# Rounding through int16 and int8 in a fused cross-attention and ternary FFN layer, with W_down prepared apart and a re-planned instruction order

## The chip, the cores and the metric

One NeuronCore of a Trainium2 chip runs the whole kernel. The metric is the device time in microseconds (us) of one execution. PE is the matmul engine, PEld its weight loads, DVE the vector engine, ACT the scalar engine, POOL the GpSimd engine, SP the engine that issues all transfers of this kernel.

## The reference

For each of 32 batches `x[b]` (128x512) and a context of the same shape, all float32:

```
x = x + xattn(layernorm(x), ctx)      # 8 heads; scores 512x512 per head, RoPE on half of each head
x = x + ffn(layernorm(x))             # 512 -> 2048 -> 512

act_quant(v):    s = 128 / clip(max|v|, 1e-5);   clip(round(v*s), -128, 127) / s     # per token
weight_quant(w): s = 1 / clip(mean|w|, 1e-5);    clip(round(w*s), -1, 1) / s         # ternary
ffn(x) = bitlinear(fwht(silu(bitlinear(x, w_gate)) * bitlinear(x, w_up)), w_down)
bitlinear(x, w) = act_quant(x) @ weight_quant(w).T                                   # fwht: Hadamard over 2048
```

Attention treats the 128 rows as channels and the 512 columns as positions, so one batch has 8 heads of 512x512 scores. Rounding is to the nearest integer in three places: the two activation quantizations and the three weights (1 MB of float32 per quarter, 4 MB each).

## The kernel before: work, staging and order

The work of a batch is cut into some thirty generators (`s_load`, `s_a`, ... `s_dn`), each of which yields what it needs next: a buffer ("get"), an event ("on"), or an engine with an estimated duration. `Plan.run` plays all generators against each other when the program is built: it keeps a clock for every engine, and among the steps that could start first on an engine it takes the one of lowest rank, given by the table `CFG` (one number per generator for the middle batches, one with `.h` for the first four and one with `.z` for the last four, plus `T` per batch). [...] Transfers, all on SP's one queue, have a length and a latency there (`DMA`, and the numbers behind `yield "dma"`). `Plan` also keeps DVE steps marked `"port"` and POOL steps from overlapping in its own clock.

Per batch, the attention runs as two units of four heads. For each unit PE makes eight groups of scores for the row maxima (`s_mpe`, L726), which DVE reduces (`s_mdve`, L741); the maxima go to DRAM and back as extra rows of the query tile (L772, L777); PE makes the scores again, transposed and with the maxima subtracted (`s_epe`, L796); ACT takes the exponential (`s_eact`, L809), and PE multiplies by the values (`s_eav`, L830). The score buffers `pS` and `pT` exist once each. The unit's sums go through DRAM, are normalized (`s_o`, L939 on POOL), projected (L948) and added to `x` (L880).

The FFN: `s_o2` normalizes, quantizes (L975 and L978) and transposes; `s_gpe`/`s_upe` multiply by W_gate and W_up (L1013); `s_gact` (silu, L1043), `s_udve` (L1068) and `s_bf` (butterflies on POOL, L1097) follow, then transposes (`s_zt`, L1117), a split into a high and a low part (`s_hi` L1129, `s_lo` L1140) and the last Hadamard factor (`s_hm`, L1156/L1157). `s_yv` copies to SBUF (L1171), `s_am` finds the token maximum (L1184 to L1223), `s_q` scales on POOL (L1232), `s_q1` and `s_q2` round (L1242, L1256), and `s_dn` multiplies by W_down (L1274) and adds the residual (L1280).

How before rounds: adding 12582912 to a float32 number leaves it rounded to an integer, and a later step takes the constant off again.

```
975   nc.scalar.activation(w, l2, AF.Identity, bias=MAG, scale=sx)             # w in PSUM
978   nc.vector.tensor_scalar(xq, w, -MAGIC, 127.0, ALU.add, ALU.min)
1242  nc.scalar.activation(y, y, AF.Identity, bias=MAG)
1256  nc.scalar.activation(s["yq"][:, w], s["y"][:, w], AF.Relu, bias=MAG7, scale=-1.0)
1275  nc.tensor.matmul(ps, NEG, CS, start=False, stop=True)
```

L1256 holds 127 minus the rounded value, so that one Relu clips it; L1275 takes the shift of 127 out of the product with W_down's column sums `CS`, made once in `s_w4` (16 matmuls at L502, four small DVE steps and a transfer to the two rows of `CS`).

The weights are prepared while the first batches' attention runs. `s_w` loads twelve pieces of 128x2048 (1 MB, L438) into the FFN's own buffers `z0`, `z1`, `z0`, `y`. `s_w1` sums absolute values in halves (L451, all on ACT), `s_w2` scales and adds the constant (L475 on ACT, one on POOL at L477), `s_w3` clips on DVE (L485), `s_w4` takes the constant off and writes fp8 on ACT (L493). The first FFN matmul (L1013 of batch 0) waits until all three weights are ready; the first L1274 waits for `CS`.

Of the kernel before, what the change touches and what calls it, by code (L numbers as in the profile page):

```python
# [13 lines left out]
F8 = mybir.dt.float8e4  # L14
AF = mybir.ActivationFunctionType
# [5 lines left out]
MAGIC = 12582912.0  # L21
EPS = 1e-5
# [3 lines left out]
    "a": 17204.8,  # L26
    "a.h": 56888.9,
    "a.z": 14936.6,
    "a2": 4110.6,
    "a2.h": 10733.7,  # L30
    "a2.z": 4091.9,
    "a3": -1064.4,
    "a3.h": 4876.9,
    "a3.z": 2422.1,
    "am": 4773.1,
    "am.h": 13803.0,
    "am.z": -44218.1,
    "bf": 3144.9,
    "bf.h": 24712.8,
    "bf.z": 19590.3,  # L40
    "const": 14934.4,
    "const.h": 15491.8,
    "const.z": 4076.0,
    "dn": 4293.7,
    "dn.h": 4871.1,
    "dn.z": 21179.4,
    "eact": -36632.4,
    "eact.h": -37814.4,
    "eact.z": -1863.9,
    "eav": 11135.5,  # L50
    "eav.h": 4223.8,
    "eav.z": 32251.8,
    "epe": -40145.6,
    "epe.h": -40187.6,
    "epe.z": -39869.7,
    "gact": 23899.5,
    "gact.h": -26090.9,
    "gact.z": -36563.3,
    "gpe": 56880.8,
    "gpe.h": 18311.9,  # L60
    "gpe.z": 6005.8,
    "hi": -25784.5,
    "hi.h": -26246.1,
    "hi.z": 4960.2,
    "hm": -21491.6,
    "hm.h": -24541.6,
    "hm.z": -28755.2,
    "init": -37791.2,
    "init.h": -23577.8,
    "init.z": -24582.5,  # L70
    "lo": 1897.6,
    "lo.h": 4758.2,
    "lo.z": -37078.3,
    "load": 23789.4,
    "load.h": 4770.3,
    "load.z": -31350.6,
    "mdve": 1736.2,
    "mdve.h": 4251.6,
    "mdve.z": -25448.7,
    "mfin": -25604.8,  # L80
    "mfin.h": 4075.5,
    "mfin.z": 6355.4,
    "mpe": -26070.7,
    "mpe.h": -37503.9,
    "mpe.z": -21599.3,
    "o": -25785.8,
    "o.h": 35362.7,
    "o.z": -786.3,
    "o2": -37005.1,
    "o2.h": -41684.7,  # L90
    "o2.z": -24211.2,
    "q": 13848.2,
    "q.h": -39189.8,
    "q.z": 4318.1,
    "q1": 11956.7,
    "q1.h": 4753.0,
    "q1.z": 21160.0,
    "q2": 1023.0,
    "q2.h": -21667.4,
    "q2.z": -23754.1,  # L100
    "st": -47909.0,
    "st.h": -35889.1,
    "st.z": 21989.2,
    "u": 26418.5,
    "u.h": 5310.5,
    "u.z": 24337.0,
    "udve": 18718.4,
    "udve.h": 12493.6,
    "udve.z": -34405.8,
    "upe": 29615.8,  # L110
    "upe.h": 19928.1,
    "upe.z": 14589.9,
    "v": 27752.8,
    "v.h": 57650.1,
    "v.z": 53459.6,
    "w": 35469.7,
    "w.h": -19469.2,
    "w.z": 18308.4,
    "w1": 24353.6,
    "w1.h": 18083.3,  # L120
    "w1.z": -34718.8,
    "w2": 28388.6,
    "w2.h": 5547.9,
    "w2.z": 12473.5,
    "w3": 31248.0,
    "w3.h": 19526.9,
    "w3.z": 3962.9,
    "w4": 25647.7,
    "w4.h": 6555.5,
    "w4.z": 20517.4,  # L130
    "yv": -26156.9,
    "yv.h": 11959.1,
    "yv.z": 33180.6,
    "zt": 13824.7,
    "zt.h": 15480.3,
    "zt.z": -26679.3,
    "T": 5.6,
    "eps": 0.019,
    "pen": 9.6,
    "stick": 4685.6,  # L140
    "epspe": 0.21,
# [5 lines left out]
    "xq": 1, "xqT": 2, "pf": 3, "z0": 2, "z1": 1, "hl": 2, "y": 1, "yq": 2, "ot": 1,  # L147
# [155 lines left out]
def xattn_ffn(  # L303
# [37 lines left out]
    MAG = const.tile([128, 1], F32, name="MAG")  # L341
    nc.vector.memset(MAG, MAGIC)
    NMAG = const.tile([128, 1], F32, name="NMAG")
    nc.vector.memset(NMAG, -MAGIC)
    MAG7 = const.tile([128, 1], F32, name="MAG7")
    nc.vector.memset(MAG7, MAGIC + 127.0)
# [10 lines left out]
    CW = const.tile([128, 388], F32, name="CW")  # L357
    WQ, WK, WVT, BRP, MASK = CW[:, 0:128], CW[:, 128:256], CW[:, 256:384], CW[:, 384:386], CW[:, 386:387]
    NEGC = CW[:, 387:388]
# [15 lines left out]

    ob = const.tile([128, 1], BF, name="ob")
    nc.vector.memset(ob, 1.0)
    NEG = const.tile([2, 128], BF, name="NEG")
    CS = const.tile([2, 512], BF, name="CS")
# [30 lines left out]
    def s_init():  # L410
        yield "on", "cw"
        yield "dve", 0.2
        nc.vector.tensor_scalar(NEG, ones[0:2, :], NEGC[0:2], None, ALU.mult)
        z = zeros[:, :, None].to_broadcast([128, 2, T])
        for i in range(4):
            yield ("dve", "pool"), (1.13, 1.4), "port"
            E[p.eng].tensor_scalar(kss[i], z, MASK, None, ALU.add)
            p.mark("ks", i)
# [10 lines left out]
    WR = ("z0", "z1", "z0", "y")  # L429

    def s_w():
        for n in range(12):
            m, k = divmod(n, 4)
            src = srcs[m][0][k]
            yield "get", WR[n % 4]
            yield "dma", 2.9
            w = fp.tile([128, 2048], F32, name=WR[n % 4], bufs=2 if WR[n % 4] == "z0" else 1)
            nc.sync.dma_start(out=w.rearrange("p (j i) -> p j i", j=4) if m == 2 else w, in_=src)  # L438
            WT[n] = w
            p.marks["w", n] = p.done  # L440
            p.now = p.done - 2.9

    def s_w1():
        for m in range(3):
            for n in range(4 * m, 4 * m + 4):
                yield "on", "w", n
                for h in range(2):
                    yield ("act", "dve"), (1.1, 1.13)
                    w, a = WT[n][:, bass.ts(h, 1024)], acc[:, 2 * n + h : 2 * n + h + 1]
                    if p.eng == "act":  # L450
                        nc.scalar.activation(AB, w, AF.Abs, accum_out=a)  # L451
                    else:
                        nc.vector.tensor_reduce(a, w, AX.X, ALU.add, apply_absolute_value=True)
            yield "get", "pf"
            yield "pe", 0.1
            pw = ps_f.tile([128, 512], F32, name="pf")
            nc.tensor.matmul(pw[:, 0:8], ones, acc[:, 8 * m : 8 * m + 8], start=True, stop=True)
            yield "dve", 0.1
            sw = SW[:, m : m + 1]
            nc.vector.tensor_reduce(sw, pw[:, 0:8], AX.X, ALU.add)  # L460
            p.put("pf")
            yield "dve", 0.1
            nc.vector.tensor_scalar(sw, sw, 1.0 / (NI * 128 * 512), EPS, ALU.mult, ALU.max)
            yield "dve", 0.1
            nc.vector.reciprocal(SC[:, m : m + 1], sw)
            p.mark("sw", m)

    def s_w2():
        for n in range(12):
            m = n // 4  # L470
            yield "on", "sw", m
            yield ("act", "pool", "dve"), (1.95, 2.7, 1.25), "port"
            w = WT[n]
            if p.eng == "act":
                nc.scalar.activation(w, w, AF.Identity, bias=MAG, scale=SC[:, m : m + 1])  # L475
            else:
                E[p.eng].tensor_scalar(w, w, SC[:, m : m + 1], MAGIC, ALU.mult, ALU.add)  # L477
            p.mark("w2", n)

    def s_w3():  # L480
        for n in range(12):
            yield "on", "w2", n
            yield ("dve", "pool"), (1.2, 2.7), "port"
            w = WT[n]
            E[p.eng].tensor_scalar(w, w, MAGIC - 1.0, MAGIC + 1.0, ALU.max, ALU.min)  # L485
            p.mark("w3", n)

    def s_w4():
        for n in range(12):
            m, k = divmod(n, 4)  # L490
            yield "on", "w3", n
            yield "act", 1.95
            nc.scalar.activation(srcs[m][1][:, k, :], WT.pop(n), AF.Identity, bias=NMAG, saturate=False)  # L493
            p.put(WR[n % 4])
            if k == 3:
                p.mark("wr", m)
        yield "get", "y"
        yield "get", "pf"
        yield "pe", 3.5
        pc = ps_f.tile([128, 512], F32, name="pf")  # L500
        for j in range(NI):
            nc.tensor.matmul(pc[0:1, :], ob, WDQ[:, j, :], start=(j == 0), stop=(j == NI - 1))  # L502
        yield "dve", 0.6
        w = fp.tile([128, 2048], F32, name="y")
        ca, cb = w[0:1, 0:512], w[0:1, 512:1024].bitcast(BF).rearrange("p (a f) -> p a f", a=2)
        nc.vector.tensor_scalar(ca, pc[0:1, :], 1.0 / 64.0, MAGIC, ALU.mult, ALU.add)
        yield "dve", 0.6, "port"
        nc.vector.tensor_scalar(cb[:, 0], ca, -MAGIC, None, ALU.add)
        yield "dve", 0.6, "port"
        nc.vector.tensor_scalar(ca, ca, -MAGIC, -64.0, ALU.add, ALU.mult)  # L510
        yield "dve", 0.6
        nc.vector.tensor_tensor(cb[:, 1], pc[0:1, :], ca, ALU.add)
        p.put("pf")
# [503 lines left out]
    def s_gpe():  # L1017
        for b in range(NB):
# [3 lines left out]
            if b == 0:  # L1022
                yield "on", "wr", 2
# [330 lines left out]
```

## Time and profile before

| | us |
|---|---|
| median of 3 runs (lowest to highest) | 1439.01 (1437.6 to 1448.16) |
| the profiled execution, its whole time | 1444.41 |
| its span, first to last instruction | 1442.5 |
| PE busy | 1353.4 (94%) |
| ACT busy | 1189.0 (82%) |
| DVE busy | 1179.0 (82%) |
| POOL busy | 994.7 (69%) |
| moved by transfers | 214.15 MB, mean 148 GB/s |

How to read it: "busy" is the time an engine executes instructions. The tables by stage give this for stretches of the span, with the mean clock that was granted to PE (1.00 is full speed). In the lists of waits a line names the instruction that waited, the one that ended the wait, the total, how many times, and the longest. In a timeline a row is one instruction or a run of them: start, length, engine, line, operation, output<-inputs, shapes, count.

### The profile page before, as it was taken

To read this page: it belongs to the slowest core of one execution; us is meant where nothing else is said; L and a number is where in the kernel's file an instruction comes from. 1 tells how busy PE (TensorE), PEld (TensorE's weight loads), DVE (VectorE), ACT (ScalarE), POOL (GpSimd) and SP (SyncE) were. 2 spreads that over 40 slices of the span, in tenths; PEclk is the share of its full clock that TensorE was granted. 3 is DMA by queue.
4 is the path that set the end of the run, shared out by engine and by line. 5 is a ranking of instruction groups with operands and counts; after the bars stand their busy time and mean duration, and the time that the engine had idled before them with its cause. 6 is when DMAs were issued, how large, how long until landed. Compare 5 with 4: busy or idle time off the path is not lost.

```text
span 1442.5 us, 21845 instructions
## 1 busy us (share of the span) xinstructions
PE 1353.4 (94%) x7454; PEld 529.8 (37%) x7454; DVE 1179.0 (82%) x1759; ACT 1189.0 (82%) x1574; POOL 994.7 (69%) x781
## 2 busy tenths in 40 slices
PE   3788899999999999999999999999999999999875
PEld 2222233433334333333333344333333343433332
DVE  2875878888898889888888888888888888886784
ACT  5688978888888888888888888888888888889643
POOL 3122229977777777887777787887777788769550
PEclk7596899999999999999999999999999999999986
DMA  8967555555445555555545555555554554321000
GB/s 285 282 201 245 158 159 160 151 152 143 134 147 163 171 171 174 161 153 148 136 134 154 171 167 175 168 162 156 137 141 140 161 166 153 95 65 49 21 15 15
DMA packets 136315, 214.15 MB, mean 148 GB/s; under 512 B 36746, under 2 KB 38924, under 8 KB 135180
## 3 DMA queue, kind: packets, MB, share of 16 engines
q1 hardware_dynamic: 136204, 212.75, 49.7%
q8 instruction: 59, 0.97, 0.3%
q14 instruction: 52, 0.43, 0.1%
HBM read 106.94 MB, written 93.31 MB: 139 GB/s over the span
## 4 chain that ended last, share of the span: by engine, by line
PE 84%; DVE 7%; ACT 4%; DMA 2%; issue 2%; POOL 0%; SPq 0%; ACTq 0%; DVEq 0%; POOLq 0%
PE pav L830 17%; PE pf L1013 15%; PE pT L796 14%; PE pS L726 10%; PE pf L1274 8%; PE pf L1117 4%; PE pf L556 4%; PE pf L1156 3%; ACT P L809 2%; DVE M L741 2%; PE pf L1157 2%; PE pf L948 2%; PE pf L636 2%; DVE ya L1184 1%; PE pf L1275 1%
## 5 line engine op out<-in xcount | busy, mean ns | idle before, releaser
L741 DVE TENSOR_REDUCE M<-pS 128x2 f32<-128x1024 f32 x488 | 595.0, 1219 | 105.0 <-PE pS L726 103.1
L1097 POOL TENSOR_TENSOR z<-z 128x512 f32<-128x512 f32 x491 | 619.0, 1283 | 68.5 <-DVE z L1068 48.5
L809 ACT ACTIVATE P<-pT 128x1024 f32<-128x1024 f32 x512 | 523.2, 1022 | 148.2 <-PE pT L796 146.4
L830 PE MATMUL pav<-P,va 128*32 128x512 f32 x2048 | 283.6, 625 | 0.0
L796 PE MATMUL pT<-qs,ks 50*128 50x512 f32 x1024 | 259.0, 500 | 17.1 <-ACT P L809 16.5
L726 PE MATMUL pS<-ks,qs 48*128 48x512 f32 x976 | 227.2, 458 | 14.8 <-DVE M L741 9.9
L796 PEld LDWEIGHTS pT<-qs,ks 50*128 50x128 f32 x1024 | 98.1, 188 | 240.3 <-ACT P L809 149.9
L1232 POOL TENSOR_TENSOR y<-y,YB 128x1024 f32<-128x1024 f32 x60 | 140.9, 2369 | 34.9 <-ACT YB L1218 34.9
L1013 PEld LDWEIGHTS <-xqT 128*128 128x128 bf16 x1024 | 91.8, 100 | 155.7 <-issue 84.8
L726 PEld LDWEIGHTS pS<-ks,qs 48*128 48x128 f32 x976 | 95.3, 190 | 117.8 <-issue 39.6
L532 POOL TENSOR_TENSOR arstd<-arstd,MHALF 128x1 f32<-128x1 f32 x32 | 18.6, 580 | 170.4 <-DVE arstd L529 134.8
L1013 PE MATMUL pf<-WGQ,xqT 128*128 128x512 fp8e4 x512 | 133.4, 386 | 1.0 <-ACT z L1043 0.6
L1274 PE MATMUL pf<-WDQ,yq 128*128 128x512 fp8e4 x512 | 125.4, 389 | 8.6 <-ACT yq L1256 8.5
L1184 DVE TENSOR_REDUCE ya<-y 128x128 f32<-128x1024 f32 x64 | 127.1, 1986 | 6.6 <-ACT y L1171 6.3
L1013 PE MATMUL pf<-WUQ,xqT 128*128 128x512 fp8e4 x512 | 127.0, 381 | 0.1
L1068 DVE TENSOR_TENSOR z<-z,pf 128x512 f32<-128x512 f32 x128 | 84.6, 675 | 12.9 <-PE pf L1013 8.7
L1140 DVE TENSOR_TENSOR lo<-pf,hi 128x512 fp32r<-128x512 f32 x128 | 85.7, 675 | 6.0 <-ACT hi L1129 5.9
L1043 ACT ACTIVATE z<-pf,tk 128x512 f32<-128x512 f32 x128 | 83.7, 685 | 7.4 <-PE pf L1013 4.7
L1129 ACT CAST hi<-pf 128x512 fp32r<-128x512 f32 x128 | 74.6, 588 | 17.9 <-PE pf L1117 17.9
L1171 ACT COPY y<-pf 128x512 f32<-128x512 f32 x128 | 71.9, 585 | 13.6 <-PE pf L1157 13.3
L1117 PE MATMUL pf<-CM,z 128*128 128x128 f32 x512 | 82.0, 286 | 0.0
L1274 PEld LDWEIGHTS <-yq 128*128 128x128 bf16 x512 | 46.1, 99 | 89.7 <-ACT yq L1256 22.5
(129 smaller groups left out, 1791.5 us busy)
## 6 DMA issues: line engine op xcount, KB each, us to landing
xd<-X SPq DMA_DIRECT2D x128, 512.0 KB
qs<-xd SPq DMA_DIRECT2D x128, 192.0 KB
ks<-xd SPq DMA_DIRECT2D x128, 192.0 KB
ud<-U SPq DMA_DIRECT2D x62, 256.0 KB
xt<-x SPq DMA_DIRECT2D x32, 256.0 KB
ct<-cx SPq DMA_DIRECT2D x32, 256.0 KB
RR<-R SPq DMA_DIRECT2D x64, 128.0 KB
xr<-x SPq DMA_DIRECT2D x32, 256.0 KB
```

The costliest lines, as they stand in the source:

```text
L726: nc.tensor.matmul(ps[e], qs[w, t, bass.ts(qt, 128)], ks[w, t, :], start=True, stop=True)
L741: nc.vector.tensor_reduce(m, ps[2], AX.X, ALU.max)
L796: nc.tensor.matmul(ps[:, e], ks[w, t, bass.ts(kt, 128)], qs[w, t, :], start=True, stop=True)
L809: nc.scalar.activation(P, TQ[u, n], AF.Exp, scale=0.25)
L830: nc.tensor.matmul(av[32 * h : 32 * h + 32, :], va[:, kt, 4 * hf + h, :], P[:, e], start=(kt == 0), stop=(kt == 3),)
L1013: nc.tensor.matmul(ps, xqT[:, k, :], W[:, k, bass.ts(c, 512)], start=(k == 0), stop=(k == 3))
L1097: E[p.eng].tensor_tensor(ix(dv, k), ix(av, 0), ix(av, 1), o)
L1117: nc.tensor.transpose(ps[:, i, :], st[b]["z"][:, bass.ts(4 * c + i, 128)], EYE)
L1140: nc.vector.tensor_tensor(t, F.pop(("z", b, c)), F["hi", b, c].bitcast(F32), ALU.subtract)
L1184: nc.vector.tensor_reduce(ya[:, h], s["y"][:, 8 * h : 8 * h + 8].rearrange("p j t -> p t j"), AX.X, ALU.max, apply_absolute_value=True,)
L1232: E[p.eng].tensor_tensor(y, y, st[b]["YB"].to_broadcast([128, 8, 128]), ALU.mult)
L1274: nc.tensor.matmul(ps, s["yq"][:, j, :], WDQ[:, j, :], start=(j == 0), stop=False)
```

## The change

Rounding is left to the conversion that an engine makes when it writes an integer type.

- `s_o2`: ACT writes `l2*sx` as int16 into SBUF (`xi`), DVE clips it from there to bf16. The PSUM buffer between them goes.
- `s_q1`, `s_q2`: ACT copies `y` to int16 (`yi`, a new buffer, one), which frees `y` there; DVE, no longer ACT, clips `yi` to `yq` in bf16.
- `s_dn`: L1275, `NEG`, `CS` and all that made them go; `s_am`'s last factor changes sign.
- Weights: three steps become two: scale to int8 (`w_scale`; all 14 on ACT in the built order) and clip from int8 to fp8 (`w_clip`, on DVE). The int8 pieces lie in the two halves of the `yi` buffer. W_gate and W_up are loaded into `z0`, `z1`, `z0` and, in two halves, into the `yq` buffers. W_down goes through `y` alone, and twice: four loads for the sum of absolute values, four again for scaling (eight loads of 1 MB in place of four).
- The first FFN matmul waits for W_gate and W_up alone, the first L1274 for W_down. `yi` is handed to batch 0 when all weights are done.
- All of `CFG` has new numbers, a `wd` entry and other `T`, `eps`, `pen`, `stick`, `epspe`; the lengths and latencies behind many `yield "dma"` are larger. So the order of instructions differs on every engine, from the first transfers on.

```diff
-MAGIC = 12582912.0
-    "T": 5.6, "eps": 0.019, "pen": 9.6, "stick": 4685.6, "epspe": 0.21,
+    "T": 573.1, "eps": 0.239, "pen": 38.0, "stick": 11286.1, "epspe": 0.192,
...
+    WP = [(m, k, 0, 2048, r) for m in range(2) for k, r in enumerate(("z0", "z1", "z0"))]
+    WP = [x for m in range(2) for x in WP[3 * m : 3 * m + 3] + [(m, 3, 1024 * h, 1024, "yq") for h in range(2)]]
...
+    def w_scale(w, wi, m, n):
+        yield ("act", "dve", "pool"), (0.2 + 0.88 * n / 1024, 0.15 + 1.07 * n / 1024, 0.3 + 2.7 * n / 1024), "port"
+        if p.eng == "act":
+            nc.scalar.activation(wi, w, AF.Identity, scale=SC[:, m : m + 1])
+        else:
+            E[p.eng].tensor_scalar(wi, w, SC[:, m : m + 1], None, ALU.mult)
+
+    def w_clip(wi, o, n):
+        yield "dve", 0.1 + 1.0 * n / 1024
+        nc.vector.tensor_scalar(o, wi, 1.0, -1.0, ALU.min, ALU.max, saturate=False)
...
+    def s_wd():
+        yield "on", "st", 1
+        for n in range(8):
+            ph, k = divmod(n, 4)
+            yield "get", "y"
+            yield "dma", 3.5
+            w = fp.tile([128, 2048], F32, name="y", bufs=1)
+            nc.sync.dma_start(out=w.rearrange("p (j i) -> p j i", j=4), in_=srcs[2][0][k])
+            p.now = p.done
+            if ph:
+                yield "on", "wi"
+                yield "get", "wi"
+                wi = WI.pop(0)
+                yield from w_scale(w, wi, 2, 2048)
+                p.put("y")
+                yield from w_clip(wi, srcs[2][1][:, k, :], 2048)
+                WI.append(wi)
+                p.put("wi")
+            else:
+                yield from abs_sum(w, 16 + 2 * k, 2048)
+                p.put("y")
+            if n == 3:
+                yield from scale(2)
+        p.mark("wr", 2)
+        yield "on", "wr", 1
+        p.put("yi")
...
-            yield "get", "pf"
-            yield "act", 0.75
-            w = ps_f.tile([128, 512], F32, name="pf")
-            nc.scalar.activation(w, l2, AF.Identity, bias=MAG, scale=sx)
-            yield "dve", 0.6
+            yield "act", 0.6
+            xi = xp.tile([128, T], I16, name="xi", bufs=1)
+            nc.scalar.activation(xi, l2, AF.Identity, scale=sx)
+            p.put("l2")
+            yield "dve", 0.35, "port"
             xq = xp.tile([128, T], BF, name="xq", bufs=1)
-            nc.vector.tensor_scalar(xq, w, -MAGIC, 127.0, ALU.add, ALU.min)
+            nc.vector.tensor_scalar(xq, xi, 127.0, None, ALU.min)
...
             if b == 0:
-                yield "on", "wr", 2
+                yield "on", "wr", 1
             yield "get", "z0"
...
-                nc.scalar.activation(y, y, AF.Identity, bias=MAG)
+                nc.scalar.copy(st[b]["yi"][:, w], st[b]["y"][:, w])
                 p.mark("q1", b, hf)
+            p.put("y")
...
-                yield "act", 1.05
+                yield "dve", 0.45, "port"
...
-                nc.scalar.activation(s["yq"][:, w], s["y"][:, w], AF.Relu, bias=MAG7, scale=-1.0)
+                nc.vector.tensor_scalar(s["yq"][:, w], s["yi"][:, w], 127.0, None, ALU.min)
...
             if b == 0:
-                yield "on", "cs"
+                yield "on", "wr", 2
...
-                    nc.tensor.matmul(ps, s["yq"][:, j, :], WDQ[:, j, :], start=(j == 0), stop=False)
-            nc.tensor.matmul(ps, NEG, CS, start=False, stop=True)
+                    nc.tensor.matmul(ps, s["yq"][:, j, :], WDQ[:, j, :], start=(j == 0), stop=(j == NI - 1))
```

## Prediction

> **What bounds the kernel now.** I read the page's busy times and slices first, then the table by stage, the waits of the stretch in which PE has gaps, and PE's timeline in the steady part.
>
> ```profile
> PE 1353.4 (94%) x7454; PEld 529.8 (37%) x7454; DVE 1179.0 (82%) x1759; ACT 1189.0 (82%) x1574; POOL 994.7 (69%) x781
> ...
> PE   3788899999999999999999999999999999999875
> ...
> PEclk7596899999999999999999999999999999999986
> ```
>
> PE is the bound from about 200 us to 1320 us. Outside of that it has gaps, and early on a granted clock below full. The stages (PE, PEld, DVE, ACT, POOL busy, then clock, transfer share, GB/s):
>
> ```profile
> 0.00:40.00 40.00, 15.93 (x66) 8.27 (x67) 13.06 (x34) 25.27 (x34) 13.05 (x17) 0.72 0.85 292
> ...
> 80.00:100.00 20.00, 16.67 (x100) 5.71 (x98) 16.75 (x27) 17.68 (x23) 5.06 (x4) 1.00 0.43 131
> 100.00:120.00 20.00, 15.30 (x79) 5.60 (x79) 14.04 (x20) 18.75 (x21) 5.51 (x5) 0.82 0.96 314
> 120.00:140.00 20.00, 17.43 (x71) 4.45 (x65) 6.98 (x10) 15.02 (x21) 7.06 (x6) 0.50 0.66 214
> 140.00:160.00 20.00, 16.51 (x93) 6.06 (x91) 16.80 (x25) 18.16 (x23) 1.83 (x2) 0.91 0.74 243
> 160.00:180.00 20.00, 15.69 (x79) 4.49 (x75) 15.28 (x21) 18.20 (x18) 7.41 (x5) 0.83 0.36 80
> 180.00:200.00 20.00, 18.06 (x89) 6.59 (x87) 14.11 (x23) 14.49 (x16) 1.81 (x2) 0.83 0.73 218
> 400.00:440.00 40.00, 40.00 (x236) 15.80 (x232) 35.03 (x52) 34.70 (x48) 31.89 (x26) 1.00 0.52 155
> 1320.00:1360.00 40.00, 34.57 (x168) 12.87 (x167) 22.45 (x41) 28.70 (x38) 28.28 (x22) 0.91 0.14 43
> 1360.00:1400.00 40.00, 32.80 (x146) 15.27 (x144) 33.64 (x54) 24.36 (x35) 20.48 (x14) 0.91 0.02 8
> ```
>
> In the steady part PE has no gap and the others have 5 us or more in 40. From 80 to 200 us PE is idle 120 - 99.66 = 20.3 us while ACT is busy over 18 of 20 us in three of six stretches: it carries the weights' steps beside the exponentials. Who ended PE's waits there (the list for 100 to 150 us, then for 150 to 200 us; columns: total us, times, longest):
>
> ```profile
> PEld pT L796 <- ACT P L809: 16.4, 13, 2.2
> ...
> PE pT L796 <- ACT P L809: 7.3, 8, 1.3
> ```
>
> ```profile
> PEld pS L726 <- DVE M L741: 11.4, 10, 2.0
> ...
> PEld pT L796 <- ACT P L809: 8.6, 10, 2.0
> ...
> PE pS L726 <- DVE M L741: 4.3, 5, 1.7
> PE pT L796 <- ACT P L809: 3.8, 4, 1.7
> ```
>
> ACT's exponentials end 16.4 + 7.3 + 8.6 + 3.8 = 36.1 us of these waits. DVE's maxima end 11.4 + 4.3 and 4.6 in three small rows (1.8, 1.7, 1.1), 20.3 in all. ACT's share is 36.1 / 56.4 = 0.64.
>
> **The change part by part.** The sum is made against the profiled execution: 1444.41 us, of which 1442.5 are span; the median of the runs is 5.4 us below it.
>
> *L1275.* PE's timeline in the steady part:
>
> ```profile
> 473.90 1.90 PE L1274 MATMUL pf<-WDQ,yq 128*128 128x512 fp8e4 x8
> 475.74 0.38 PE L1275 MATMUL pf<-CS,NEG 2*128 2x512 bf16 x1
> 476.05 0.50 PE L796 MATMUL pT<-qs,ks 50*128 50x512 f32 x2
> ```
>
> From its start to the next start are 0.31 us; eight matmuls followed by L796 take 1.83 us elsewhere too (L1013 at 503.09, next at 504.92), as the eight L1274 do here. So 32 x 0.31 = 10.0 us of a full PE go. The order of the other matmuls changes as well. I priced every group in both orders by the start-to-start intervals of its kind and neighbours between 210 and 1320 us: 1326.6 us before, 1319.9 after. So the new mix of switches gives back 10.0 - 6.7 = 3.3 us; bounds 0 and 6.7 (for over a quarter of the groups the new neighbours do not occur in the trace, and kinds alone priced them). A batch then takes 39.8 us in place of 40.13.
>
> *CS.* L502 stands on the chain of waits for 3.54 us at 188.18: 3.5 us go; its four DVE steps (0.7, 0.7, 0.4, 0.4 us), the transfer of 2 KB and five memsets of 0.06 us lie beside PE work.
>
> *q2 moves.* ACT loses 64 x 1.138 us (L1256), 2.3 per batch, and gains nothing: the int16 write of L1242 and of L975 is priced at their rows (1.138, 0.769). ACT is under PE by 5 us per 40, so this gives 0 in the steady part. DVE gains two clips. The trace has no int16; the nearest form is L485 (SBUF to SBUF, one scalar step, 1.21 us for 2048), so 0.61 for 1024, between 0.27 (L768, the smallest tensor step) and 1.22 (L1232 on DVE). L978 (0.68, from PSUM) becomes 0.3 by the same rate. DVE per batch: 35.1 + 1.2 - 0.4 = 35.9 of 39.8: room of 3.9 us. Behind each clip the next L741 is queued, and PE's L726 waits for that one, since `pS` exists once. In the new steady order PE has at least 1.7 us from one pS group to the next, the same as in the old order, which ran without a gap. So I take 0, with that room as the cover.
>
> By the table of modes in the Trainium skill (VectorE: DVE Perf Modes, the section on cycles for N=2048) an all-16-bit clip of 1024 would take an estimated 0.43 us, DVE 35.6 per batch; the sum would be the same.
>
> *A lock that speaks against it.* POOL's R step took 2.16 us at 176.66, where it takes 1.27 otherwise, while L485 held DVE:
>
> ```profile
> 176.47 1.22 DVE L485 TENSOR_SCALAR z<-z 128x2048 f32<-128x2048 f32 x1
> ```
>
> ```profile
> 175.31 1.27 POOL L662 TENSOR_TENSOR RR<-RR,ROPE 128x512 f32<-128x512 f32 x1
> 176.66 2.16 POOL L664 TENSOR_TENSOR R<-R,RR 128x512 f32<-128x512 f32 x1
> ```
>
> So a clip from SBUF and a POOL step exclude each other. The old steady part has no such DVE step; the new one has three per batch beside a POOL that is busy 31.9 of 40. Waiting for the rest of a POOL step, 0 to 1.28 us each (2.37 behind L1232), adds 0 to 3 x 1.28 = 3.8 us per batch to DVE: just inside its 3.9. I take the half, 1.9, hidden.
>
> The Trainium skill (SBUF, "Who interferes with whom") says the later of the two blocks for the whole instruction, an int16 clip included. By it all three could wait a whole POOL step, and DVE would stand at 39.7 of 39.8, nearly a second bound; by the half it costs nothing.
>
> *The start.* CW, ROPE and CM now precede x, three pieces of W_gate precede RR in place of two, and the first piece of W_up precedes the first score tiles. Ahead of the last transfer of unit 0's tiles stand 11.3 MB in place of 9.8 (sizes of the issue list). At 292 GB/s the 1.5 MB cost 5.1 us on the chain to the first scores, where PE has nothing else: +5; bounds 0 (the chain R to X sets it) and 9 (projection later too).
>
> *80 to 200 us.* Of the weights' steps ACT has from 95 us on 8 x 2.0 (L493), 6 x 2.09 (L475) and 8 x 1.24 (L451), 38.5 us. In the new order only W_down's sums (9.9) and four scalings (8.4) are left there, 18.3: ACT loses 20 of 105 us. The clips to fp8 are DVE's: 12 x 1.21 by L485, up to 12 x 2.44 by L1232, most of them done by the second unit; before, it had 12 x 1.26 there. Nothing is priced for DVE here at the lower price. PE gets back ACT's share of its idle time, 0.64 x 20.3 = 13 us; bounds 0 (DVE or transfers are late next) and 20.3. W_down's four extra MB cost 4 / 0.29 = 14 us of a queue that is idle 47 us between 40 and 200 us: hidden, unless it stands ahead of a small transfer (3.6 us per MB). Batch 0's L1156 waits for `y`, that is for W_down's eighth load; if it comes late PE stands up to 3.6 + 2.1 us, and `yi` holds batch 0's L1242 until all weights are done, on ACT with exponentials behind it. The order puts the last scaling 41 ACT places ahead of that, so 0.
>
> *The tail.* On the last batch's chain L1256's second half gets 0.5 shorter and L978 0.4: -1; its new order may give or take 6.
>
> Sum: -10.0 + 3.3 - 3.5 + 5 - 13 - 1 = -19.2, or 1425 for the profiled execution. On the median: 1439.0 - 19.2 = 1420.
>
> **The rivals.** (a) Transfers, not ACT, hold the early attention: the share is 0.96 at 100 to 120 us, and 4 MB come on top. Against it: 0.36 and 0.43 in two stretches with the same PE idle time. Then 13 is not gained and the start costs 9: 1420 + 13 + 4 = 1437. (b) The lock decides in the steady part: each of three waits costs PE half a POOL step, 0.64 us, as L741 comes late: 3 x 0.64 x 29 batches = 56, 1476. It decides from 19.2 / 29 = 0.7 us of PE gap per batch. For it: POOL's share; against: DVE's room. (c) More comes back: all of 20.3, and the half clock at 120 to 140 us, which cost 17.43 / 2 = 8.7, by ACT's share 5.6: 1420 - 7 - 6 = 1407.
>
> **How the numbers follow.** Forecast 0.50 (1410 to 1430), (a) 0.22, (b) 0.13, (c) 0.15. About 1% (1424.6 to 1453.4) is what a measurement tells from no change. The forecast lies under 1424.6 in 0.44 of its 0.50, with (c) 0.59, rounded to 0.6 faster; the rest of it and (a) make 0.27 the same, (b) 0.13 slower. The range runs from all terms at their good ends, 1439 - 10 - 3.5 - 20.3 - 6 = 1399, to (a) with the tail's 6 and L1156's 5.7 on top, 1449.
>
> **What would show it.** Right: steady batches of 39.8 us (L1274 to L1274), PE at 40.00 of 40; idle PE from 80 to 200 us near 7 us and fewer us of "pT <- ACT P"; first L726 near 42 in place of 37 us. Wrong: "pS <- DVE M" growing in the steady part with clips longer than 0.6 us, or PE's early waits going from ACT to DVE or to transfers.

## The result

The changed kernel takes 1460.3 us (median of 4 runs, 1459.18 to 1461.71), the kernel before 1441.27 us beside it (4 runs, 1437.6 to 1448.16): a ratio of 1.0127, 95% interval 1.0085 to 1.0169. It is slower by 1.3%, where 1420 us were forecast. The profiled execution took 1460.03 us, with a span of 1457.2.

### The profile page after: what moved, and what is told of

It is laid out like the page before. It is cut to its first block, busy times and chain, and to the rows that moved or that the text cites. A ratio compares the mean times of both kernels' runs of the same rounds, so it can differ in the third digit from the quotient of the medians.

```text
span 1457.2 us, 21717 instructions
## 1 busy us (share of the span) xinstructions
PE 1340.4 (92%) x7406; PEld 532.5 (37%) x7406; DVE 1242.0 (85%) x1819; ACT 1113.1 (76%) x1501; POOL 999.9 (69%) x777
## 4 chain that ended last, share of the span: by engine, by line
PE 70%; DVE 15%; ACT 8%; DMA 3%; issue 2%; POOL 1%; SPq 0%; ACTq 0%; DVEq 0%; POOLq 0%
PE pav L842 14%; PE pf L1023 13%; PE pT L808 12%; PE pS L738 8%; PE pf L1291 7%; DVE M L753 5%; ACT P L821 4%; PE pf L1127 3%; PE pf L1166 3%; DVE yq L1273 3%; PE pf L648 2%; PE pf L1167 2%; PE pf L960 2%; PE pf L568 1%; DMA RR<-R 1%
## 5 line engine op out<-in xcount | busy, mean ns | idle before, releaser
L1194 DVE TENSOR_REDUCE ya<-y 128x128 f32<-128x1024 f32 x64 | 126.3, 1974 | 13.1 <-ACT y L1181 10.8
L1023 PEld LDWEIGHTS <-xqT 128*128 128x128 bf16 x1024 | 86.2, 98 | 131.8 <-issue 61.2
L1291 PE MATMUL pf<-WDQ,yq 128*128 128x512 fp8e4 x512 | 123.9, 387 | 4.6 <-DVE yq L1273 3.2
L671 POOL TENSOR_TENSOR R<-R,ROPE 128x512 f32<-128x512 f32 x32 | 41.9, 1309 | 71.0 <-DMA RR<-R 71.0
L1181 ACT COPY y<-pf 128x512 f32<-128x512 f32 x128 | 74.1, 582 | 14.2 <-PE pf L1167 13.8
L1139 ACT CAST hi<-pf 128x512 fp32r<-128x512 f32 x128 | 74.2, 586 | 11.7 <-PE pf L1127 10.8
L1127 PEld LDWEIGHTS pf<-CM,z 128*128 128x128 f32 x512 | 59.0, 147 | 54.0 <-issue 33.3
```

The source lines that it names most:

```text
L1023: nc.tensor.matmul(ps, xqT[:, k, :], W[:, k, bass.ts(c, 512)], start=(k == 0), stop=(k == 3))
L1127: nc.tensor.transpose(ps[:, i, :], st[b]["z"][:, bass.ts(4 * c + i, 128)], EYE)
L1194: nc.vector.tensor_reduce(ya[:, h], s["y"][:, 8 * h : 8 * h + 8].rearrange("p j t -> p t j"), AX.X, ALU.max, apply_absolute_value=True,)
L1291: nc.tensor.matmul(ps, s["yq"][:, j, :], WDQ[:, j, :], start=(j == 0), stop=(j == NI - 1))
```

## The profile after the change

The page's busy times and slices, as the prediction showed them of the kernel before:

```profile
PE 1340.4 (92%) x7406; PEld 532.5 (37%) x7406; DVE 1242.0 (85%) x1819; ACT 1113.1 (76%) x1501; POOL 999.9 (69%) x777
...
PE   3698899998999999999999999999999999999775
...
PEclk7579999998999999999999999999999999999997
```

PE is busy 13 us less and the span is 14.7 us longer, so PE's idle time grew by 28 us. The mean granted clock over the whole span is the same (0.953, before 0.950); it is lower in the stretch from 200 to 480 us and higher ahead of it. DVE's busy time went up by 63 us and ACT's down by 76. Two rows of the table by stage (PE, PEld, DVE, ACT, POOL busy, then clock, transfer share, GB/s):

```profile
120.00:140.00 20.00, 16.67 (x101) 5.31 (x93) 10.12 (x18) 16.48 (x22) 5.58 (x5) 0.91 0.91 270
...
400.00:440.00 40.00, 37.98 (x201) 15.50 (x198) 32.38 (x45) 30.87 (x41) 25.01 (x21) 0.91 0.51 150
```

By the six rows from 80 to 200 us PE is idle 15.6 us (20.3 before), and the clock is higher on the mean of the six (0.91, before 0.82): 0.50 at 120 us has become 0.91, though 1.00 at 80 us has become 0.73. From 400 to 440 us, where PE was at 40.00 of 40, it now has gaps and a clock of 0.91. The changed kernel in three wide windows, and then the kernel before:

```profile
200.00:480.00 280.00, 268.58 (x1479) 104.77 (x1480) 231.94 (x335) 214.72 (x286) 202.32 (x159) 0.95 0.52 156
480.00:1040.00 560.00, 549.32 (x3205) 218.05 (x3204) 523.99 (x750) 460.51 (x625) 447.81 (x346) 1.00 0.54 155
1040.00:1320.00 280.00, 273.52 (x1517) 111.28 (x1515) 247.00 (x372) 221.01 (x302) 225.52 (x172) 1.00 0.41 120
```

```profile
200.00:480.00 280.00, 278.61 (x1595) 107.85 (x1591) 239.80 (x354) 240.35 (x322) 228.47 (x181) 1.00 0.51 150
480.00:1040.00 560.00, 559.46 (x3231) 220.40 (x3230) 489.57 (x726) 485.38 (x655) 445.38 (x349) 1.00 0.54 155
1040.00:1320.00 280.00, 278.87 (x1582) 111.43 (x1581) 240.44 (x351) 240.14 (x324) 219.88 (x170) 1.00 0.44 129
```

PE's idle time grew from 1.4 to 11.4 us in the fill (200 to 480 us), from 0.5 to 10.7 in the steady part (480 to 1040), and from 1.1 to 6.5 from 1040 to 1320 us. The timeline of DVE and then of PE in one steady batch of the changed kernel:

```profile
576.06 1.22 DVE L753 TENSOR_REDUCE M<-pS 128x2 f32<-128x1024 f32 x1
...
577.32 2.85 DVE L1273 TENSOR_SCALAR yq<-yi 128x1024 bf16<-128x1024 int16 x2
580.08 1.22 DVE L753 TENSOR_REDUCE M<-pS 128x2 f32<-128x1024 f32 x1
```

```profile
578.19 0.39 PE L738 MATMUL pS<-ks,qs 48*128 48x512 f32 x2
...
580.09 0.49 PE L808 MATMUL pT<-qs,ks 50*128 50x512 f32 x2
581.35 0.50 PE L738 MATMUL pS<-ks,qs 48*128 48x512 f32 x2 [0.77 <-DVE M L753]
581.79 1.90 PE L1291 MATMUL pf<-WDQ,yq 128*128 128x512 fp8e4 x8
583.62 0.50 PE L808 MATMUL pT<-qs,ks 50*128 50x512 f32 x2
```

The two clips L1273 stand in a row. The scores for the next maximum were begun at 578.19, but DVE gets to it at 580.08. PE needs the one `pS` again and stands 0.77 us. The same gap comes in each steady batch, which takes 40.47 us where 39.8 was forecast. The rest is as forecast: the eight L1291 take 1.83 us to the next start, and L1275 is gone.

To see where the time went I use the lag: the time of a group on PE less the PE work done up to then, priced by start-to-start intervals as in the prediction (1326.6 us in all before, 1319.9 after). The growth of the lag in each stretch, us, from the profiled executions (labels of the runs are explained below):

| | work | to 200 | 200-480 | 480-1040 | 1040-1320 | 1320 to end | span |
|---|---|---|---|---|---|---|---|
| before | 1326.6 | 61.7 | 1.8 | 0.6 | 2.2 | 49.6 | 1442.5 |
| after | 1319.9 | 46.9 | 23.0 | 9.0 | 8.8 | 49.6 | 1457.2 |
| e1, no clips of yq | 1319.9 | 47.1 | 12.2 | -3.2 | 12.0 | 46.5 | 1434.5 |
| e5, clips apart | 1319.9 | 47.2 | 18.3 | -3.7 | 11.0 | 53.5 | 1446.2 |
| e11, order alone | 1319.9 | 48.7 | 16.0 | -4.6 | 8.0 | 48.5 | 1436.5 |
| e7, old order, no L1275 | 1380.2 | in the work | 3.5 | 1.7 | 2.6 | 48.5 | 1436.5 |

After less before: -6.7 of PE work, -14.8 up to 200 us, +21.2, +8.4, +6.6, 0: +14.7 us. The prediction had the first two (the second as 5 - 13 - 3.5 = -11.5) and nothing for the next three. (A negative growth means that a batch needs less than its priced work: 39.45 us in place of 39.8.) The prices are uncertain by some us in all (the prediction gave 0 to 6.7 for the new mix), so differences of 2 us or less say nothing. For e7 the work and the first stretch stand as one number, 1380.2 us, 8.1 less than in the kernel before (1326.6 + 61.7).

## The experiments

Theory 1: the clips on DVE make the maxima late; by their length (1b), by the exclusion with POOL, or by their place (1c). Theory 2: the new order loses time where batches start and end. Theory 3: the weights' new preparation does.

**e1: without the clips of yq.**

```
-  st[b]["yi"] = fp.tile([128, NI, 128], I16, ...); nc.scalar.copy(st[b]["yi"][:, w], ...)
+  st[b]["yq"] = fp.tile([128, NI, 128], BF, ...);  nc.scalar.copy(st[b]["yq"][:, w], ...)
-  nc.vector.tensor_scalar(s["yq"][:, w], s["yi"][:, w], 127.0, None, ALU.min)
```

> The changed kernel in its own order; L1256 writes yq as bf16 at once and the two clips L1273 are left out (so y is neither rounded nor bounded at 127). It takes away two DVE steps per batch (2.77 us in the steady batch) and adds none. Theory 1 (the clips wait for POOL's steps and make the maxima L753 late): the one PE gap per batch, 0.77 us of 40.47, goes; steady batch 39.8 us or a little less, PE 40.0 of 40, total 1460 - 29 x 0.65 = 1441 or less, and part of the 23 us lost from 200 to 480 us comes back too (1430 to 1441). Theory 2 (the new order is the cause wherever the clips are): a gap of 0.5 us or more per batch stays, total 1453 to 1461.

Measured: 1439.33 us, ratio to the kernel before 1.0011 (0.9991 to 1.0031); the steady batch is 39.47 us. Its row of the wide window:

```profile
480.00:1040.00 560.00, 558.75 (x3274) 221.33 (x3271) 499.00 (x741) 469.76 (x636) 453.61 (x354) 1.00 0.55 158
```

PE's idle time in the steady part falls from 10.7 to 1.3 us. The clips, priced at nothing, cost 0.0116 x 1440 = 17 us by the two ratios, 22.7 by the two spans: 10.8 in the fill and 12.2 in the steady part. Of the 10.8 some 5 lie from 340 to 360 us, where the clock is 1.00 in e1 and 0.66 in the changed kernel (last section); that the clips made it so is not shown, since e11, without them, has 0.68 there. But the kernel without the clips is no faster than the kernel before, where 1420 us were forecast, so a second cause of about 20 us is left.

**e2: clips that leave POOL's ports alone.**

```
-  nc.vector.tensor_scalar(s["yq"][:, w], s["yi"][:, w], 127.0, None, ALU.min)
+  nc.vector.tensor_scalar(s["yq"][:, w], s["yi"][:, w], 127.0, None, ALU.min, ALU.add, accum_out=DUMP)
   (L990 in the same way)
```

> The changed kernel in its own order and with the same arithmetic; L1273 and L990 also write a sum of their elements that nobody reads. The clip takes the DVE about as long as in the changed kernel or longer by itself. By the Trainium skill (SBUF, 'Who interferes with whom') this form does not take the port pair that POOL uses. Theory 1, if it is the exclusion that counts: the clips take one duration every time (somewhere from 0.5 to 1.3 us, without the spread of 0.41 to 1.52), POOL's L1107 falls from 1.46 back to 1.25 us beside them, the PE gap per batch falls to 0.3 us or less, 1440 to 1451. Theory 1b, if it is only the DVE's time that counts (a clip of 1.2 us is as bad as a wait of 1 us): the batch stays at 40.4 us, 1456 to 1464. Theory 2 (order): as 1b.

Measured: 1462.93 us, ratio 1.016 (1.0135 to 1.0185); steady batch 40.18 us. The clips' rows between 480 and 1040 us, first of the changed kernel, then of e2, then of e8 (told below), which has the plain form at other places:

```profile
L1273 DVE TENSOR_SCALAR yq<-yi 128x1024 bf16<-128x1024 int16 x28 | 39.8, 1461 | 0.0
```

```profile
L1274 DVE TENSOR_SCALAR_CACHE_REDUCE yq<-yi 128x1024 bf16<-128x1024 int16 x28 | 34.0, 1214 | 1.7
```

```profile
L1245 DVE TENSOR_SCALAR yq<-yi 128x1024 bf16<-128x1024 int16 x28 | 11.5, 411 | 0.0
```

The exclusion is there: the plain clip takes 0.41 us where POOL is idle and 1.46 beside POOL's products, so about a microsecond of it is waiting. The Trainium skill (SBUF — State Buffer, "Who interferes with whom") lets the later of the two block; the rows agree. The form that by that page doesn't contend takes 1.21 us each time, because it is slower by itself. The gap per batch falls from 0.77 to 0.5 us and the total doesn't. So it isn't the exclusion as such that costs PE time, but how long DVE is away from the maxima, whatever the reason.

**e3: without the weights' clips.**

```
-  yield from w_scale(WT.pop(n), wi[:, 0:w], m, w)
+  yield from w_scale(WT.pop(n), srcs[m][1][:, k, c : c + w], m, w)      # W_down's in the same way
-  nc.vector.tensor_scalar(o, wi, 1.0, -1.0, ALU.min, ALU.max, saturate=False)
```

> The changed kernel in its own order; the scaling L463/L465 writes fp8 into the weights' tiles at once and the DVE clips L469 are left out (so the weights are neither rounded to -1, 0, 1 nor bounded). Twelve DVE steps' worth of 2048 elements (14 in number, 1.1 to 1.75 us each, some 18 us in all) go, all before 290 us. Theory 3 (W_gate's, W_up's and W_down's DVE steps are what the fill loses): of the 21 us that the changed kernel loses against the one before between 200 and 480 us, half or more come back, 1440 to 1450. Theory 1 and 2: the loss of 200 to 480 us stays, since most of it falls after the last weight step; 1455 to 1461.

Measured: 1456.55 us, ratio 1.0129 (1.0094 to 1.0164), not to be told from the changed kernel. The fill's lag grows by 16.3 us in place of 23.0; most of the difference lies in the stretch from 320 to 360 us, of which the last section tells. Theory 3 in this form falls.

**e4: the old priorities.**

```
-  CFG = {... of the changed kernel ...}
+  CFG = {... of the kernel before ..., "wd": 25647.7, "wd.h": 6555.5, "wd.z": 20517.4}
```

> The changed kernel's code and prices with the priorities of the kernel before (W_down's own stream, which that one did not have, gets those of its last weight step); so another order. Theory 2 (the new priorities cost the steady part and the fill): steady batch 39.8 to 40.0 us, total under 1445. Theory 1 (clips beside POOL): the clips still take 0.41 to 1.5 us, a PE gap per batch of 0.5 us or more stays or grows, steady batch 40.3 us or more; total 1450 to 1480.

Measured: 1644.31 us, ratio 1.1422 (1.1355 to 1.1489), outside both. From 480 to 1040 us the down matmuls of one batch begin 39 to 69 us behind those of the last, and PE is idle 34 of the 560 us. The priorities were made for other steps and other prices, and another set of steps with them gives quite another order. This run tells nothing of the causes; it shows that an order can't be judged by carrying the table over.

**e5: the second clip behind the next maximum.**

```
   nc.vector.tensor_reduce(m, ps[2], AX.X, ALU.max)      # L753
+  late()     # issues a clip that waits in LATE; called too ahead of a new `yi` and of the second half of the down matmuls
...
-  nc.vector.tensor_scalar(s["yq"][:, w], s["yi"][:, w], 127.0, None, ALU.min)
+  if hf == 0: nc.vector.tensor_scalar(s["yq"][:, w], s["yi"][:, w], 127.0, None, ALU.min)
+  else: LATE.append((s["yq"][:, w], s["yi"][:, w]))
```

> The changed kernel with one step of the DVE moved: the second clip L1273 of a batch stands behind the next maximum L753 and no longer right behind the first clip. The DVE does the same work. Theory 1c (the place counts: two clips of 1.42 us in a row between two maxima are longer than PE's other work there, 0.77 us longer): the gap per batch falls to 0.2 us or less, steady batch 39.5 to 39.8 us in place of 40.47, total 1438 to 1446. Theory 1b (the DVE's time as a whole counts, 37 to 38 of 40 us): the batch stays at 40.3 to 40.5 us, 1456 to 1461.

Measured: 1449.11 us, ratio 1.0048 (1.0026 to 1.007); steady batch 39.45 us. DVE and PE at the place of the gap:

```profile
570.98 1.42 DVE L1283 TENSOR_SCALAR yq<-yi 128x1024 bf16<-128x1024 int16 x1
...
571.85 0.39 PE L738 MATMUL pS<-ks,qs 48*128 48x512 f32 x2
...
572.32 1.21 DVE L753 TENSOR_REDUCE M<-pS 128x2 f32<-128x1024 f32 x1
...
573.46 0.41 DVE L1267 TENSOR_SCALAR yq<-yi 128x1024 bf16<-128x1024 int16 x1
...
574.09 0.40 PE L738 MATMUL pS<-ks,qs 48*128 48x512 f32 x2
```

The maximum starts at 572.32, behind one clip, and ends before PE asks for `pS`. PE has no gap, although DVE is busy 523.55 of 560 us, as in the changed kernel (523.99). So theory 1b falls for the steady part: the place decides, not DVE's sum. The total is 11 us below the changed kernel by the two ratios, and 3 us above the range expected of theory 1c.

**e6: the clip on ACT.**

```
-  yi = fp.tile(..., I16, ...)                 -> L1256 writes int16
+  yi = fp.tile(..., I16, ...) read as int8    -> L1256 writes int8
-  nc.vector.tensor_scalar(s["yq"][:, w], s["yi"][:, w], 127.0, None, ALU.min)
+  nc.scalar.copy(s["yq"][:, w], s["yi"][:, w])
```

> The changed kernel in its own order; L1256 writes int8 in place of int16 (which bounds the value), and what was the clip on the DVE is a copy from int8 to bf16 on ACT at the same place, some 1.05 us each. Theory 1 (the DVE's clips are what the steady part loses): as without the clips, batch 39.5 to 39.8 us, total 1437 to 1446. Rival (ACT, at 32.8 of 40 us, then makes the exponentials late by its 2.1 us more): gaps behind 'pT <- ACT P' in the steady part, batch 40.2 us or more, 1452 to 1464.

Measured: 1491.8 us, ratio 1.0353 (1.0316 to 1.039), beyond the rival's number; steady batch 41.03 us. The one row of PE's waits in e6 from 480 to 1040 us:

```profile
PE pT L808 <- ACT P L821: 21.0, 14, 1.5
```

That is 1.5 us in each of 14 batches, behind an ACT that is busy 478 of 560 us. The two copies stand in a row on ACT (1.98 us from 621.59 us on in one batch), right before the exponential of 623.47 us that ends one of these waits; they do on ACT what the two clips do on DVE. The 14 batches are 0.56 us longer each than in the changed kernel, 8 of the 29 us by which the span is longer; where the other 21 come from was not looked into.

**e7 and e8: the kernel before without the correction.** One part of the change alone, in the old order, with the weights as before: e7 with the clip on ACT, e8 on DVE.

```
-  nc.tensor.matmul(ps, NEG, CS, start=False, stop=True)                      # L1275
-  16 matmuls L502 and four DVE steps for CS
-  nc.scalar.activation(y, y, AF.Identity, bias=MAG)                          # L1242
+  nc.scalar.copy(st[b]["yi"][:, w], st[b]["y"][:, w])                        # e7 int8, e8 int16
-  nc.scalar.activation(s["yq"][:, w], s["y"][:, w], AF.Relu, bias=MAG7, scale=-1.0)   # L1256
+  e7: nc.scalar.copy(s["yq"][:, w], s["yi"][:, w])
+  e8: nc.vector.tensor_scalar(s["yq"][:, w], s["yi"][:, w], 127.0, None, ALU.min)
```

> The kernel before in its own order with one part of the change alone: the correction matmul L1275, its sums L502 and their DVE steps are out, L1242 writes int8 and L1256 is a copy from int8 to bf16, both on ACT as before. Nothing goes to the DVE, the weights are prepared as before. The prediction's first step: 32 x 0.31 = 10 us and 3.5 us at L502 go, steady batch 40.13 to 39.8 us, total 1438 - 13.5 = 1424. Rival (the time of L1275 is hidden or comes back at the switches, as 3.3 of 10 did in the new order's pricing): 1430 to 1438.

> As the run on ACT, but with int16 and the clip on the DVE, at the places where L1256 stood in the order of the kernel before; there 7 or so DVE steps lie between the two clips of a batch. The DVE then has 35 + 2.0 to 2.9 = 37 to 38 us of 39.8. Theory 1c (the place counts): no gap, like the run on ACT within 5 us, 1422 to 1430. Theory 1b (the DVE's time as a whole counts): a gap of 0.5 us or more per batch, batch 40.3 us or more, 1438 to 1445.

Measured: e7 1434.54 us, ratio 0.9944 (0.9926 to 0.9961), faster than both kernels; e8 1440.4 us, ratio 0.9985 (0.9959 to 1.0012). In e7 PE goes from the start of the eight down matmuls to the next group in 1.83 us. The shortest steady batches take 39.82 us in both (forecast 39.8), but the median ones 39.99 and 40.05, where the kernel before has 40.15. The part is worth 8 us in e7, not 13.5: the total lies in the range of the rival that part of it comes back. e8's total lies in the range named for theory 1b, and the clips on DVE cost 6 us more there than on ACT by the two ratios, whose intervals just touch; but its batches are not the 40.3 us of that theory. In e8 PE never waits for `pS` in the steady part: maxima stand between the two clips of a batch, each clip takes 0.41 us, and the first falls into a pause of POOL (DVE's row, then POOL's rows around it):

```profile
587.41 0.40 DVE L1245 TENSOR_SCALAR yq<-yi 128x1024 bf16<-128x1024 int16 x1
```

```profile
586.03 0.55 POOL L519 TENSOR_TENSOR orstd<-orstd,MHALF 128x1 f32<-128x1 f32 x1
588.67 2.50 POOL L1084 TENSOR_TENSOR z<-z 128x512 f32<-128x512 f32 x2 [2.09 <-DVE z L1055]
```

The changed kernel is e8 with the weights' new preparation, the new steps of `s_o2` and the new order, and takes 20 us more.

**e9: without W_down's stream.**

```
-  nc.sync.dma_start(out=w..., in_=srcs[2][0][k]); abs_sum, scale(2), w_scale, w_clip of W_down
+  nc.gpsimd.memset(WDQ..., 0.0); nc.vector.memset(SW[:, 2:3], 1.0)       # at the start
```

> The changed kernel in its own order; the whole stream of W_down is left out: its eight transfers L512 of 1 MB, its sums, its scale, four scalings and four clips. WDQ is filled with zeros once at the start and its scale is 1 (so the output lacks the FFN's last product). Everything else stands where it stood. Theory 3b (W_down's separate preparation, with its 8 MB and its hold on y and yi, is what the fill loses between 200 and 480 us): the lag's rise from 200 to 360 us falls from 17 to under 8 us, total 1445 to 1452. Theory 2 (the order of the batches' steps in the fill, attention first and the FFN in clumps): the rise stays within 4 us of what it was, total 1453 to 1461.

Measured: 1452.52 us, ratio 1.0093 (1.0061 to 1.0125). The fill's lag grows by 13.3 us in place of 23.0; of this difference 5 to 6 us lie in one stretch, 320 to 360 us, in which the clock differs (see the last section). The time lies between the two ranges, and so does the lag's growth from 200 to 360 us (45.7 to 56.0: 10.3). e11 settles it.

**e10: both clips behind a maximum.** As e5, but the first clip waits too, save in the last three batches.

```
-  if hf == 0: nc.vector.tensor_scalar(s["yq"][:, w], s["yi"][:, w], 127.0, None, ALU.min)
-  else: LATE.append((s["yq"][:, w], s["yi"][:, w]))
+  LATE.append((hf, s["yq"][:, w], s["yi"][:, w]))      # one is issued behind each L753
+  if b >= NB - 3: late(2)
+  late(sum(x[0] <= g for x in LATE))                   # in s_dn: a clip still waiting goes ahead of its half
```

> The changed kernel with the same work; each clip L1273 stands behind a maximum L753 of its own, the first one too, in all batches but the last three (where no maxima are left to stand behind, as in the changed kernel). Theory 1c (place): steady batch 39.45 us as with the second clip alone moved; in the fill and the last stretch a part of the 10 us by which the run with the second clip moved (1449) lies above the one without clips (1439) goes too: 1441 to 1447. Rival (those 10 us are the clips' wait ahead of the down matmuls, not the maxima's): 1447 to 1452.

Measured: 1469.49 us, ratio 1.0197 (1.016 to 1.0235); steady batch 40.46 us. Outside both expectations, on the slow side. The largest of PE's waits from 480 to 1040 us, and the down matmuls that it holds up in one batch:

```profile
PE pf L1303 <- DVE yq L1266: 7.1, 14, 1.7
```

```profile
579.21 1.90 PE L1303 MATMUL pf<-WDQ,yq 128*128 128x512 fp8e4 x8 [0.43 <-DVE yq L1266]
```

DVE is busy 14 us less than in the changed kernel (509.76 of 560), and the batch is as long. The wait has only changed its name: the first clip is now late for the down matmuls (7.1 us), and the split `lo` is late too (4.7 us in 14 waits, by the same list). The first clip must come before the maximum and the second behind it: e5, which has this, has neither wait. The 10 us by which e10's total lies above the changed kernel's are not in the steady part, where PE is idle 12.2 us in place of 10.7.

**e11: the order alone.** The edits of e1, e3 and e9 in one, and L990 out as well:

```
-  xi = xp.tile([128, T], I16, ...); nc.scalar.activation(xi, l2, AF.Identity, scale=sx)
-  nc.vector.tensor_scalar(xq, xi, 127.0, None, ALU.min)
+  xq = xp.tile([128, T], BF, ...);  nc.scalar.activation(xq, l2, AF.Identity, scale=sx)
```

> The changed kernel in its own order, with all that the change adds beside the order left out at once: the clips L1273 and L990 (ACT writes bf16), the weights' clips L469 (the scaling writes fp8), and W_down's whole stream (WDQ zeros, scale 1). What is computed is therefore cut by these parts. Left are the order and the lower number of steps. Theory 2 (the order by itself loses time where batches start and end): the lag still rises by 8 us or more from 200 to 360 us and by 8 or more from 1040 to 1320 us (before: 2 in each), total 1428 to 1438. Theory 3c (the added steps of DVE, ACT and the queue together, none of them alone): both rises fall to 4 us or less, total 1410 to 1425.

Measured: 1437.49 us, ratio 0.9987 (0.9959 to 1.0014). The lag grows by 14.2 us from 200 to 360 us and by 8.0 from 1040 to 1320; theory 2 holds. With these added steps left out the kernel is only as fast as the one before, although its steady batch is 39.47 us in place of 40.13. Beside the order it still has the new loads and the one scaling step of W_gate and W_up. Some 5 of the 14.2 us lie from 340 to 360 us, where the clock is 0.68; without them the rise is still above the 8 us of theory 2.

```profile
200.00:480.00 280.00, 269.51 (x1517) 104.64 (x1517) 225.89 (x323) 217.28 (x294) 204.15 (x162) 0.97 0.52 154
480.00:1040.00 560.00, 559.84 (x3272) 222.39 (x3268) 492.52 (x729) 470.91 (x636) 448.67 (x352) 1.00 0.56 159
1040.00:1320.00 280.00, 273.59 (x1526) 112.27 (x1523) 234.54 (x346) 222.10 (x304) 223.71 (x172) 1.00 0.39 113
```

PE is idle 10.5 us in the fill (the first row) and 6.4 from 1040 to 1320 us, nearly as in the changed kernel (11.4 and 6.5), and 0.2 between. In the changed kernel's fill no gate or up matmul starts from 320 to 360 us (32 start from 280 to 320 us and 40 from 360 to 400; in the kernel before 32 in each of the three stretches), and PE has attention work there; e11 has the same 32, 0 and 40; the changed kernel's first down matmul comes at 284 us though its clips begin at 267.6. PE's largest wait in e11 from 200 to 360 us is "pT <- ACT P" (5.3 us, 10 times). That this unevenness is the reason is read from the traces and was not tried.

**e12: as e5, with the second clip at its old place in the last four batches.**

```
   LATE.append((s["yq"][:, w], s["yi"][:, w]))
+  if b >= NB - 4: late()
```

> As the run with the second clip behind the next maximum, but in the last four batches the second clip stands where the changed kernel has it. If the moved clip delays the down matmuls in the end, where few maxima are left to stand behind, 4 to 6 us of that run's 1449 go: 1443 to 1446. If not, 1447 to 1451.

Measured: 1447.92 us, ratio 1.0051 (1.003 to 1.0073): the moved clip isn't what e5 lacks against e1. That difference, 5 us by the two ratios and 10 by the medians, stays open; in the two profiles (11.7 us by the spans) it lies in the stretch with the lower clock at 340 us (about 5) and behind 1320 us (7).

## Why the prediction was wrong

- **L1275 and the switches (-10 + 3.3): right in the new order.** The batch without gaps is 39.82 us in the old order and 39.45 in the new one, even below 39.8. The pricing of the new neighbours was a third of a microsecond too high per batch. In the old order the part with L502 gave 8 of its 13.5 us (e7); most batches there stay above 39.82.
- **q2's clips (0): the step that failed.** It took DVE's room of 3.9 us per batch as the cover, and "at least 1.7 us from one pS group to the next" as enough. Both are sums or least distances over a batch. The two clips stand in a row (2.85 us), between two maxima, where PE has 2.4 us of other work from the start of one pS group (578.19) to when it stood (580.58). The cost is 17 us by the ratios of e1. DVE's sum was not the error: with the 1.9 us of waiting the prediction had 37.8 us per batch, and 37.9 were measured (523.99 of 560). Rival (b) had the right engine and the right threshold, "0.7 us of PE gap per batch"; 0.77 was measured. It put the gap down to waits for POOL, which e2 shows to be one of two ways to the same length, and its price of 3 x 0.64 us was too high, since only one place in the batch decides.
- **The clip's duration (0.61 taken, from 0.27 to 1.22, and half a POOL step of waiting).** By itself 0.41; beside POOL 1.46, that is 1.05 of waiting and not 0.64: POOL works back to back there, and the DVE waits for most of a step. The clip of `s_o2`, L990, priced at 0.3, takes 0.27 to 1.19 us in the steady part.
- **Start +5: right.** The first scores begin at 39.9 us in place of 35.1.
- **80 to 200 us (-13) and L502 (-3.5): right in sum, and by luck.** With the start they make -11.5; the lag at 200 us fell by 14.8. But PE's idle time fell only from 20.3 to 15.6 (7 was named), and the rest came as clock. ACT's part of the waits did not shrink either: "pT <- ACT P" in PE and its loads from 100 to 200 us went from 36.1 to 19.7 + 5.7 + 13.5 + 4.1 = 43.0. So the mechanism named for the 13 us, less ACT work and shorter waits for ACT, is not what the trace shows.
- **What had no step, the second failure: 200 to 480 and 1040 to 1320 us.** The prediction priced the new order by neighbours of matmuls alone, and so took for granted that PE would run without gaps outside the steady batches too, as it did in the old order. e11 puts 14.2 and 5.8 us there (growth over that of the kernel before; some 5 of the 14.2 come with the lower clock at 340 us), which eat up most of what the head, the steady part and L1275 give.
- **W_down's extra transfers (0):** not a term that decides. Without its whole stream the kernel takes 5 us less by the two ratios, whose intervals overlap, and part of that is the clock.
- **The tail (-1):** 49.6 us before and after.

## What to carry to other kernels

An engine's free time per batch is no cover for a step: lay the new instructions between the two that bound the bottleneck's next start, and ask both what stands behind them and who waits for them. Moving one of two clips behind the next maximum gave 11 us; moving both cost some 10 by the ratios (whose intervals overlap slightly), with the same work. An order that is better in the repeated part must also be read where it starts and ends, since there it can lose what it gains.

## What the runs showed of the hardware

- An int16 to bf16 clip of 128x1024 takes 0.41 us on DVE when no POOL step is running at its start and 1.36 to 1.51 in the steady part when one of POOL's products is. The waiting goes both ways: the product that POOL begins during such a clip takes 1.45 to 1.47 us, where beside e2's clips it takes 1.27 to 1.30. Over all products the mean goes only from 1.28 to 1.30 us. DVE's waiting counts as busy in the profile, so its 523.99 of 560 us hold some 29 us of waiting (28 x 1.05).
- The same clip with an accumulator takes 1.21 us whatever POOL does, and an ACT copy from int8 to bf16 1.04 us.
- The same PE idle time can bring a lower clock or not. From 320 to 360 us the changed kernel and e1 have the same busy time; the clock of the second half is 0.66 in the one and 1.00 in the other, and the lag from 340 to 360 us grows by 6.2 and by 1.2 us. The three largest gaps of PE in the first half are alike, 0.95, 0.78 and 0.58 us in the one and 0.96, 0.79 and 0.58 in the other; in the changed kernel half the clock is granted from 339.9 us on for 13.7 us, in e1 never from 300 to 400 us. What decides it is not shown. The changed kernel, then e1:

```profile
340.00:360.00 20.00, 18.04 (x87) 5.18 (x85) 12.00 (x20) 13.14 (x17) 6.84 (x5) 0.66 0.44 126
```

```profile
340.00:360.00 20.00, 18.02 (x107) 6.07 (x105) 13.16 (x20) 14.83 (x20) 7.12 (x6) 1.00 0.58 175
```
